# Fronts and merges between the batches of a scan network as threads of one plan; gate by channels

## The chip, the cores and the metric

The kernel runs on one core of a Trainium2 chip. A core has five engines with queues of their own, each in program order: PE (TensorE, matrix products), DVE (VectorE), ACT (ScalarE), POOL (GpSimd) and SP (SyncE, which here only issues DMA transfers). The metric is the device time of one execution in microseconds (us). Before the change it is 16153.37 us, the median of three runs (16113.97 to 16171.61).

## The reference, cut to what matters

Four layers work on x of 4 images, 64 x 64 tokens, 96 channels. Only layers 0 and 1 are touched by the change. Both are selective state-space layers over four directions of scan:

```python
xz = x @ in_proj_w.T                  # x is _gn(x), normalized by groups of 3 channels
xc, z = jnp.split(xz, 2, axis=-1)     # 192 channels each
xc = silu(depthwise_conv3x3(xc) + conv_b)
ys = [scan(xc in the order of direction k) for k in range(4)]
y = sum over k of w[k] * y_k restored to image order    # layer 0: w by token; layer 1: all 1
y = layernorm(y) * ln_g + ln_b        # over the 192 channels
y = y * silu(z)                       # the gate
x = x + y @ out_proj_w.T              # layer 1 adds an FFN of y as well
```

Layers 2 and 3 (attention, Fourier mixing, quantized FFNs) and the FFN of layer 1 come after, as stages of their own.

## The kernel before, in words

`Stream.run` does both scan layers as one stream of 8 batches: four images of layer 0, four of layer 1. A batch has 4 directions of 4 segments of 1024 tokens; a segment has 6 blocks of 32 channels by 4 groups of states, one tile of 128 x 1024 each. For such a tile DVE multiplies (L725) and scans (L732), ACT makes the decay (L720), POOL multiplies by C (L742), and PE spreads (L712) and gathers (L753). The preparation of the next segment (`prepare`) is woven into the slots of the current one by a `Weave`.

A batch needs a **front** before its scans and a **merge** after them. Both happen between batches: at the change from batch q-1 to q, `between` (called in `run` after `flush`, which drains the last tiles of q-1) runs `front` of batch q+1 and `merge` of batch q-1. Both are generators, and `between` advances them in turn, one `yield` each, with `front` left out on every third turn. So the order of instructions on every engine's queue is that of the fixed `yield`s. The first front runs alone before everything, the second just before the first scans; the last merge runs alone at the end.

`front` loads x in four strips of 1024 tokens and takes their statistics (L284), loads the strips again with one row above and below (`load_strip`, L271 and L279), normalizes them (L310), and then for each strip: `project` multiplies by the input weights, for xc by channels (L318, copied by L324 into a padded tile "spare") and for z by tokens (L330, silu in L335, stored to `z_tok` in DRAM); `convolve` runs the 9 taps as products with diagonal blocks of 32 x 32 (L356, `tile_position` of 3 x 4 places), silu (L370), turns the result to tokens (L376, L380), stores it (L391) and a product of it with the weights Ds (L393 and L395 on POOL, stored in L398).

`merge` goes through 8 chunks of 512 tokens. `fetch` loads the four directions' rows into the four buffers "h": plain loads (L422), or for directions 2 and 3 of layer 0 four indirect gathers each, issued by POOL (L426). `add` sums them (L448 with weights by token in layer 0, L450 in layer 1) and takes the statistics of the layernorm (L460 to L463). `gate` normalizes and multiplies by ln_g, ln_b and z: in layer 0 all on DVE (L472 to L474), in layer 1 the normalization on DVE (L478) and three products and sums on POOL (L480, L481). `leave` turns the chunk to channels (L492, L497); layer 0 multiplies by the output weights (L504), adds x (L506) and stores x1 (L508); layer 1 stores y1 (L500).

Pools hold what is shared: "h" 4 buffers, "hc" 3, "da" 4, "spare" 2, "dx", "x_in" and "yt" one, PSUM "t" 2 and "m", "u", "y" one each. "dt", "xs" and "sp_z" of the pool `seg` belong to `prepare` during the scans; "sp_z" also takes the front's product.

The later stages (`layer1_ffn`, `layer2`, `layer3`) are already written as threads of a `Plan`: a thread yields the engine it wants and the microseconds that this takes in a model, and `Plan.run` always goes on with the thread that can start first. `Rings` hands out buffers and takes them back.

Of the kernel before, what the change touches and what calls it, by code (L numbers as in the profile page):

```python
# [11 lines left out]
F32 = mybir.dt.float32  # L12
# [9 lines left out]
B = 4  # L22
HW = 64
# [121 lines left out]

class Layer:


    def __init__(self, s, a, pre, x_in):
# [9 lines left out]
        self.ln_g, self.ln_b = (k.t(w, [128, DI], pre + n) for n in ("ln_g", "ln_b"))  # L159
        nc.sync.dma_start(self.ln_g, a[pre + "ln_g"].to_broadcast([128, DI]))  # L160
        nc.sync.dma_start(self.ln_b, a[pre + "ln_b"].to_broadcast([128, DI]))
# [58 lines left out]
class Stream:  # L220
# [38 lines left out]
    def front(self, bt):  # L259

        k, nc, lay = self.k, self.nc, bt.lay
        x = lay.x_in[:, bt.b, :]
        bt.x_tok = k.t(self.dram, [L, DI], "x_tok")
        bt.dx_tok, bt.z_tok = (k.t(self.dram, [L, DI], n, bufs=3) for n in ("dx_tok", "z_tok"))
        stats = k.t(self.tmp, [C, NCH, 6], "gn_stats")
        strips = L // SEG
        tiles, pads = {}, {}

        def load(s):
            xs = k.t(self.core, [C, SEG], "da", bufs=4)  # L270
            nc.sync.dma_start(xs, x[:, s * SEG : (s + 1) * SEG])  # L271
            return xs

        def load_strip(s):

            tiles[s] = load(s), k.t(self.tmp, [C, 2, HW], "halo", bufs=2)
            for n, row in enumerate((s * 16 - 1, s * 16 + 16)):
                if 0 <= row < HW:
                    nc.sync.dma_start(tiles[s][1][:, n], x[:, row * HW : (row + 1) * HW])  # L279

        for c in range(strips):
            xs = load(c)
            for j in range(2):
                nc.vector.bn_stats(stats[:, 2 * c + j, :], xs[:, j * CH : (j + 1) * CH])  # L284
            yield
        for s in range(2):
            load_strip(s)
        mv, gn, d = (k.t(self.tmp, [C, n], t) for n, t in ((2, "gn_mv"), (2, "gn"), (1, "gn_d")))
        nc.vector.bn_aggr(mv, stats.rearrange("p c s -> p (c s)"))
        ps = k.t(self.ps, [C, 1], "m")  # L290
        nc.tensor.matmul(ps, self.gavg, mv[:, 0:1], start=True, stop=True)
        yield
        nc.vector.tensor_copy(gn[:, 0:1], ps)
        nc.vector.tensor_sub(d, mv[:, 0:1], gn[:, 0:1])
        nc.vector.scalar_tensor_tensor(d, d, d, mv[:, 1:2], op0=ALU.mult, op1=ALU.add)
        ps = k.t(self.ps, [C, 1], "m")
        nc.tensor.matmul(ps, self.gavg, d, start=True, stop=True)
        yield
        k.rstd(gn[:, 1:2], ps)

        def project(s):

            pad = pads[s] = self.spare()[:C].rearrange("p (h r w) -> p h r w", h=2, r=18)
            nc.gpsimd.memset(pad[:, :, :, 0 : HW + 2 : HW + 1], 0.0)
            r0 = s * 16
            xs, halo = tiles.pop(s)
            has = [r0 > 0, r0 + 16 < HW]
            edge = slice(0 if has[0] else 1, 2 if has[1] else 1)
            for v in (xs, halo[:, edge]):
                nc.vector.tensor_scalar(v, v, gn[:, 0:1], gn[:, 1:2], op0=ALU.subtract, op1=ALU.mult)  # L310
            for n in range(2):
                if not has[n]:
                    nc.gpsimd.memset(pad[:, :, n * 17, :], 0.0)
            for part in range(3):
                v = xs[:, part * CH : (part + 1) * CH] if part < 2 else halo[:, edge].rearrange("p r w -> p (r w)")
                ps = k.t(self.ps_t, [C, 2, CH], "t")[:, :, : v.shape[1]]
                for half in range(2):
                    nc.tensor.matmul(ps[:, half], lay.in_w[:, half * C : (half + 1) * C], v, start=True, stop=True)  # L318
                yield
                if part < 2:  # L320
                    rows = slice(1 + part * 8, 9 + part * 8)
                else:
                    rows = slice(edge.start * 17, 18, 17) if edge.stop == 2 else slice(0, 1)
                nc.scalar.copy(pad[:, :, rows, 1 : 1 + HW], ps.rearrange("p h (r w) -> p h r w", w=HW))  # L324
            stores = []
            for j in range(2):
                ps = k.t(self.ps_t, [128, 2, CH], "t")[:, :, : 2 * DI].rearrange("p a (b d) -> p a b d", d=DI)
                for t in range(4):
                    at = j * CH + t * 128
                    nc.tensor.matmul(  # L330
                        ps[:, t // 2, t % 2], xs[:, at : at + 128], lay.in_w[:, DI:], start=True, stop=True
                    )
                yield
                z = k.t(self.tmp, [128, 2, 2, DI], "z_rows", bufs=2)
                nc.scalar.activation(z, ps, AF.Silu)  # L335
                at = r0 * HW + j * CH
                to = bt.z_tok[at : at + CH, :].rearrange("(j p) d -> p j d", p=128)
                stores.append((to, z.rearrange("p a b d -> p (a b) d")))
            yield
            for to, z in stores:  # L340
                nc.sync.dma_start(to, z)
            if s + 2 < strips:
                load_strip(s + 2)

        def convolve(s):
            pad = pads.pop(s)

            two, one = k.t(self.ps_t, [128, 2, CH], "t"), k.t(self.ps, [128, CH], "m")
            ps = [two[:, 0, :], two[:, 1, :], one]
            for tap in range(9):  # L350
                dy, dx = divmod(tap, 3)
                for blk in range(C // GC):
                    mine = slice(blk * GC, (blk + 1) * GC)
                    for at in range(4):
# [4 lines left out]
                            pad[mine, half, j * 8 + dy : j * 8 + dy + 8, dx : dx + HW],  # L359
# [4 lines left out]

            for _ in range(3):
                yield
            xc = []
# [1635 lines left out]
```

## Time and profile before

| what | us |
|---|---|
| median of three runs | 16153.37 |
| the profiled execution, its time | 16120.49 |
| its span | 16118.7 |
| VectorE busy in it | 12944.4 (80%) |
| PE busy | 13409.0 (83%) |
| ScalarE busy | 8242.0 (51%) |
| GpSimd busy | 9957.1 (62%) |
| first scan begins | 392.5 |
| last scan ends | 12878.7 |

The span is the time from the first to the last instruction. The share of busy time of an engine is an average over stages with different limits; a table of windows gives it for one stretch, with the granted clock of PE and the share of time in which the 16 DMA engines were busy. In a table of waits, a row tells which engine's instruction waited for which, for how long in all, how often, and the longest time. In the groups of instructions, the first number behind the bar is busy time, the second the mean of one in ns, and behind the second bar stands the idle time before them with what ended it.

### The profile page before, as it was taken

To read this page: it belongs to the slowest core of one execution; us is meant where nothing else is said; L and a number is where in the kernel's file an instruction comes from. 1 tells how busy PE (TensorE), PEld (TensorE's weight loads), DVE (VectorE), ACT (ScalarE), POOL (GpSimd) and SP (SyncE) were. 2 spreads that over 40 slices of the span, in tenths; PEclk is the share of its full clock that TensorE was granted. 3 is DMA by queue.
4 is the path that set the end of the run, shared out by engine and by line. 5 is a ranking of instruction groups with operands and counts; after the bars stand their busy time and mean duration, and the time that the engine had idled before them with its cause. 6 is when DMAs were issued, how large, how long until landed. Compare 5 with 4: busy or idle time off the path is not lost. (4 is left out here: it accounts for less than half of the span.)

```text
span 16118.7 us, 190118 instructions
## 1 busy us (share of the span) xinstructions
PE 13409.0 (83%) x70447; PEld 4873.8 (30%) x70447; DVE 12944.4 (80%) x9690; ACT 8242.0 (51%) x14120; POOL 9957.1 (62%) x5025
## 2 busy tenths in 40 slices
PE   6888788878887888788878887888688869998877
PEld 3222222222222222222222222222222234443344
DVE  1989798979897989799979997999899956565555
ACT  3656465646564656466545654655466523332334
POOL 1888588858885888577757775777677730000123
PEclk8888888988888888888878888888788879998878
DMA  3333533353334333433343334333433320000132
GB/s 113 107 114 109 157 109 110 114 160 104 115 107 151 107 115 109 152 109 119 115 143 120 111 114 154 107 115 107 139 112 122 101 65 18 11 17 13 37 84 69
DMA packets 927836, 1675.23 MB, mean 104 GB/s; under 512 B 103206, under 2 KB 617515, under 8 KB 923132
## 3 DMA queue, kind: packets, MB, share of 16 engines
q1 hardware_dynamic: 890044, 1587.51, 31.7%
q0 software_dynamic: 36864, 75.55, 1.5%
q8 instruction: 558, 9.14, 0.2%
q14 instruction: 370, 3.03, 0.1%
HBM read 1308.00 MB, written 354.75 MB: 103 GB/s over the span
## 5 line engine op out<-in xcount | busy, mean ns | idle before, releaser
L742 POOL TENSOR_TENSOR hc<-h,bc 128x1024 f32<-128x1024 f32 x3072 | 7183.5, 2357 | 2112.6 <-DVE h L732 1681.4
L732 DVE TENSOR_TENSOR_SCAN h<-da,state,t 128x1024 f32<-128x1024 f32 x2304 | 5270.8, 2328 | 13.7 <-ACT da L720 9.6
L753 PE MATMUL y<-hc,gather_y 128*32 128x512 f32 x12288 | 4281.9, 689 | 671.4 <-POOL hc L742 506.2
L725 DVE TENSOR_TENSOR t<-u,bc 128x1024 f32<-128x1024 f32 x3072 | 3599.5, 1217 | 998.8 <-PE u L712 998.3
L720 ACT ACTIVATE da<-dts,L_A_logs 128x1024 f32<-128x1024 f32 x3072 | 3488.1, 1147 | 730.8 <-DMA dts<-dt_dram 438.4
L712 PE MATMUL u<-dtu,spread 32*128 32x512 f32 x3072 | 1881.2, 739 | 374.2 <-DVE t L725 370.2
L776 PE MATMUL y<-L_diag,zeros 96*32 96x256 f32 x5218 | 1751.8, 466 | 0.0
L732 DVE TENSOR_TENSOR_SCAN h<-da,t 128x1024 f32<-128x1024 f32 x768 | 1711.7, 2268 | 9.1 <-ACT da L720 8.4
L753 PEld LDWEIGHTS y<-hc,gather_y 128*32 128x32 f32 x12288 | 802.1, 117 | 2465.9 <-issue 1266.7
L644 PE MATMUL m<-xs,proj 96*128 96x512 f32 (+1 forms) x2048 | 1017.8, 620 | 116.7 <-ACT dt L653 60.4
L681 ACT COPY dt<-m 96x512 f32<-96x512 f32 x512 | 296.7, 579 | 1533.5 <-PE m L676 1533.5
L712 PEld LDWEIGHTS u<-dtu,spread 32*128 32x128 f32 x3072 | 597.9, 215 | 1440.1 <-issue 1101.2
L776 PEld LDWEIGHTS y<-L_diag,zeros 96*32 96x32 f32 x5218 | 617.7, 132 | 1284.8 <-issue 1158.4
L1186 POOL MEMSET padp<- 128x2448 f32 x32 | 68.5, 2141 | 1413.1 <-PE d L1226 1405.0
L1262 DVE SCALAR_TENSOR_TENSOR hcv<-padv,taps,hcv 128x2048 f32<-128x2048 f32 x384 | 902.2, 2349 | 22.3 <-ACT padv L1203 8.6
L1226 PE MATMUL d<-padp,diag 32*32 32x512 f32 x25600 | 886.2, 601 | 2.0 <-ACT hcp L1241 2.0
L676 PE MATMUL m<-sp_z,ident 96*96 96x512 f32 x1024 | 535.1, 605 | 192.7 <-ACT sp_z L670 192.7
L636 POOL TENSOR_TENSOR dtu<-sp_z,dtu 96x1024 f32<-96x1024 f32 x256 | 604.1, 2360 | 72.5 <-ACT dtu L634 70.1
L648 ACT ACTIVATE sp_z<-m,L_dtb 96x512 f32<-96x512 f32 x512 | 348.8, 681 | 545.4 <-PE m L644 527.7
L1226 PEld LDWEIGHTS d<-padp,diag 32*32 32x32 f32 x25600 | 483.3, 103 | 372.1 <-issue 199.3
L797 ACT COPY spare<-m 128x512 f32<-128x512 f32 x384 | 225.0, 586 | 713.3 <-PE m L794 712.9
L644 PEld LDWEIGHTS m<-xs,proj 96*128 96x128 f32 (+1 forms) x2048 | 322.6, 177 | 822.8 <-issue 314.2
(276 smaller groups left out, 15542.6 us busy)
## 6 DMA issues: line engine op xcount, KB each, us to landing
bc<-bc_dram SPq DMA_DIRECT2D x1024, 512.0 KB
dts<-dt_dram SPq DMA_DIRECT2D x768, 512.0 KB
dt_dram<-dt SPq DMA_DIRECT2D x256, 384.0 KB
h<-y_tok SPq DMA_DIRECT2D x192, 384.0 KB
y_tok<-spare SPq DMA_DIRECT2D x64, 768.0 KB
z_tok<-z_rows SPq DMA_DIRECT2D x64, 384.0 KB
x_tok<-y_rows SPq DMA_DIRECT2D x32, 768.0 KB
dx_tok<-sp_z SPq DMA_DIRECT2D x32, 768.0 KB
```

The costliest lines, as they stand in the source:

```text
L636: rest = lambda half: nc.gpsimd.tensor_add(r[:, half], z[:, half], r[:, half])
L644: nc.tensor.matmul(ps, proj[:, src, to], xs[:, src, cols], start=src == 0, stop=src == 1)
L676: nc.tensor.matmul(ps, k.ident[:C, :C], term[:, half, cols], start=at == 0, stop=at == 2)
L712: self.nc.tensor.matmul(seg.u[:, cols], self.spread[rows, :], seg.dtu[rows, half, cols], start=True, stop=True)
L720: self.nc.scalar.activation(da, seg.dts[cb], AF.Exp, scale=seg.bt.lay.neg_a[:, seg.kd, g : g + 1])
L725: self.nc.vector.tensor_mul(gr.t, gr.seg.u, self.bc[:, 0, gr.sg, :])
L732: self.nc.vector.tensor_tensor_scan(gr.h[:, order], gr.da[:, order], gr.t[:, order], start, op0=ALU.mult, op1=ALU.add)
L742: self.nc.gpsimd.tensor_mul(gr.hc, gr.h, self.bc[:, 1, gr.sg, :])
L753: nc.tensor.matmul(seg.y[at : at + GC, :], self.gather_y, gr.hc[:, part * CH : (part + 1) * CH], start=gr.sg == 0, stop=gr.sg == NSG - 1, ...
L776: self.nc.tensor.matmul(gr.seg.y[at : at + GC, :256], self.zeros, gr.seg.bt.lay.diag.rearrange("p h t c -> p (h t c)")[:, :256], start=Fal ...
L1226: nc.tensor.matmul(pc[i][j * 32 : (j + 1) * 32, :], diag[mine, ON_PE.index(t), tap, :], pad[mine, j * 8 + dy : j * 8 + dy + 8, dx : dx + H ...
L1262: nc.vector.scalar_tensor_tensor(to, win, wt, to, op0=ALU.mult, op1=ALU.add)
```

## The change

`Plan` and `Rings` move up in the file and get two additions: a thread can be `ahead`, which decides between threads that can start at the same time, and a ring can be cut out of a larger tile (`parts`). `front` and `merge` become sets of threads of such a plan, one for each strip's projection, convolution, statistics, edges, and one for each chunk's finish, with fetches and sums beside them. `between` is replaced by `side_by_side`, which puts the front of batch q+1, the merge of batch q-1 and the flush of the last scans (`ending`) into one plan; `fill` adds products with zeros where the model sees PE idle. At the start the fronts of batches 0 and 1 share a plan.

Beside the order, these things change: x is loaded once and kept in the four buffers "da"; z is projected by channels and stored as `z_t` (96 x 2 x 4096); the layernorm's scale and shift are applied by ACT, by channels, after the turn, and the gate's product follows there on DVE (layer 1's gate leaves POOL); direct rows of directions 0 and 1 get two buffers of their own, cut from "dt", and z two from "xs"; the bank "u" of layer 0 is held until x is added, since the output product goes into its first half; the borders of "spare" are zeroed by DVE. The loop of the convolution's products is not changed.

```diff
+    def side_by_side(self, ahead, behind=None, flush=None):
+        k, nc = self.k, self.nc
+        plan, rings = Plan(), Rings(k)
+        self.ended, self.idle = False, None
+        def ending():
+            yield "none", 1.2
+            if flush:
+                flush()
+            self.idle = k.t(self.ps_y, [128, CH], "y")
+            self.ended = True
+            yield "PE", 4.0
+        def fill():
+            if self.idle is not None:
+                data = self.layers[0].diag.rearrange("p h t c -> p (h t c)")[:, :384]
+                nc.tensor.matmul(self.idle[:GC, :384], self.zeros, data, start=True, stop=True)
+        plan.fill = fill
+        if behind:
+            plan.add(self.merge(behind, plan, rings))
+        for bt in ahead:
+            plan.add(self.front(bt, plan, rings, None if bt is ahead[0] else ahead[0]), 1)
+        plan.add(ending())
+        plan.run()
+        self.idle = None
...
-            for _ in self.front(batches[0]):
-                pass
+            self.side_by_side(batches[:2])
...
-                    flush()
+                    q = batches.index(seg.bt)
+                    if q:
+                        self.side_by_side(batches[q + 1 : q + 2], batches[q - 1], flush)
                     before = []
                     seg.bt.y_tok = [k.t(self.dram, [L, DI], f"y_tok{kd}") for kd in range(ND)]
-                    self.between(batches.index(seg.bt), batches)
...
-            flush()
-            for _ in self.merge(batches[-1]):
-                pass
+            self.side_by_side([], batches[-1], flush)
```

`Plan.run` and the start of `Plan.add`, as they are after the change (`Rings.take` and `give` as before, but for `parts`):

```python
    def add(self, work, ahead=None):
        at = self.current.at if self.current else 0.0
        if ahead is None:
            ahead = self.current.ahead if self.current else 0
        self.threads.append(SimpleNamespace(work=work, at=at, wants=("none", 0.0), ahead=ahead))
    ...
                start = max(th.at, self.free.get(th.wants[0], 0.0))
                if best is None or (start, -th.ahead) < (best[0], -best[1].ahead):
                    best = start, th
            start, th = best
            engine, us = th.wants
            if engine == "PE" and self.fill:
                for _ in range(int((start - self.free.get("PE", start)) / 1.0)):
                    self.fill()
            if engine != "none":
                self.free[engine] = start + us
                now = max(now, start)
            th.at = start + us + (0.2 if us else 0.0)
```

In `front` (one strip's load with its statistics, and z; `convolve` has the same matmuls, with `take`, `give` and costs between them):

```diff
+        def measure(s, st):
+            st.x = yield from take(self.core, [C, SEG], "da", 4)
+            yield "SP", 0.1
+            nc.sync.dma_start(st.x, x[:, s * SEG : (s + 1) * SEG])
+            yield "none", 2.5
+            yield "DVE", 1.4
+            for j in range(2):
+                nc.vector.bn_stats(stats[:, 2 * s + j, :], st.x[:, j * CH : (j + 1) * CH])
...
+            def outer(j):
+                cols = slice(j * CH, (j + 1) * CH)
+                ps = yield from take(self.ps_t, [C, 2, CH], "t", 2)
+                yield "PE", 1.8
+                for half in range(2):
+                    w = lay.in_w[:, DI + half * C : DI + (half + 1) * C]
+                    nc.tensor.matmul(ps[:, half], w, xs[:, cols], start=True, stop=True)
+                z = yield from take(self.tmp, [C, 2, CH], "z_rows", 2)
+                yield "ACT", 1.1
+                nc.scalar.activation(z, ps, AF.Silu)
...
+                nc.sync.dma_start(bt.z_t[:, :, at : at + CH], z)
...
+        works = [work for s, st in enumerate(strips) for work in (project(s, st), convolve(s, st))]
+        yield from plan.together(works)
```

In `merge`:

```diff
+        def fetch(kds):
+            if kds[0]:
+                yield lambda: self.ended
+            for n in range(NCH):
+                for kd in kds:
+                    if kd < 2:
+                        g = yield from take(None, None, "rows", 2)
+                    else:
+                        g = yield from take(self.core, [128, T, DI], "h", 4)
+                    if not lay.ordered or kd < 2:
+                        yield "SP", 0.1
+                        nc.sync.dma_start(g, rows_of(bt.y_tok[kd], n))
+                    else:
+                        yield "POOL", 5.0
+                        for j in range(T):
...
+                    plan.add(landed((n, kd), g))
...
+        def finish(n, acc, mv):
+            plan.add(load(("z", n), None, None, "z", 2, bt.z_t[:, :, cols_of(n)]))
+            yield "ACT", 1.0
+            nc.scalar.activation(mv[:, :, 1], mv[:, :, 1], AF.Sqrt, bias=k.eps)
+            yield "DVE", 1.7
+            nc.vector.reciprocal(mv[:, :, 1], mv[:, :, 1])
...
+                nc.vector.tensor_scalar(acc[:, j], acc[:, j], m, r, op0=ALU.subtract, op1=ALU.mult)
+            give(mv)
+            ps = yield from take(self.ps_u, [C, 2, CH], "u", 1)
...
+            yield "PE", 2.4
...
+            yt = yield from take(tmp, [C, 2, CH], "yt", 1)
+            yield "ACT", 1.4
+            for half in range(2):
+                g, b = lay.ln_g[:, half : half + 1], lay.ln_b[:, half : half + 1]
+                nc.scalar.activation(yt[:, half], ps[:, half], AF.Identity, bias=b, scale=g)
+            yield lambda: ("z", n) in got
+            z = got.pop(("z", n))
+            yield "DVE", 1.1
+            nc.vector.tensor_mul(yt, yt, z)
...
             if not lay.ordered:
-                yield
-                nc.sync.dma_start(self.y1[:, bt.b, cols].rearrange("(h c) t -> c h t", c=C), yt)
+                give(ps)
...
+            yield "PE", 1.6
             for half in range(2):
-                nc.tensor.matmul(ps, self.out_w[:, half, :], yt[:, half, :], start=half == 0, stop=half == 1)
...
+                nc.tensor.matmul(ps[:, 0], self.out_w[:, half, :], yt[:, half, :], start=half == 0, stop=half == 1)
+            give(yt)
+            yield lambda: ("x", n) in got
+            xs = got.pop(("x", n))
+            yield "DVE", 0.75
+            nc.vector.tensor_add(xs, xs, ps[:, 0])
+            give(ps)
```

## The prediction

> **What bounds the kernel now.** The change touches only the code that runs between the batches of the two scan layers, so I first separated those stretches. On the timeline of VectorE I took, at each change of batch, the end of the last scan (L732) and the start of the next batch's first one:
>
> ```profile
> 1802.11 4.58 DVE L732 TENSOR_TENSOR_SCAN h<-da,state,t 128x1024 f32<-128x1024 f32 x2
> ...
> 2013.48 4.45 DVE L732 TENSOR_TENSOR_SCAN h<-da,t 128x1024 f32<-128x1024 f32 x2
> ```
>
> From 1806.7 to 2013.5 us nothing is scanned: 206.8 us. The seven gaps are 206.8, 206.4, 209.0, 209.5 (each merges a layer 0 batch beside a front), 187.2, 185.0 (layer 1 merge beside a front) and 129.8 (merge alone), 1333.7 us of a span of 16118.7. Outside them lie the last merge, 135 us up to the first L1195 matmul of the next stage at 13013.9, and the start, where the first scan begins at 392.5. Everything else, 8 scan phases of 1357 to 1414 us and the last 3100 us, keeps its instructions. Next, the busy time by engine in these stretches (columns: PE, weight loads, VectorE, ScalarE, GpSimd, granted clock, DMA share, GB/s):
>
> ```profile
> 100.00:392.00 292.00, 192.02 (x2122) 103.98 (x2120) 23.70 (x45) 95.94 (x204) 38.25 (x21) 0.80 0.44 131
> 1807.00:1827.00 20.00, 5.55 (x18) 1.92 (x18) 2.69 (x6) 2.45 (x3) 10.06 (x10) 0.62 0.90 283
> ...
> 1807.00:2013.00 206.00, 118.51 (x1150) 63.75 (x1150) 110.02 (x303) 59.26 (x90) 87.13 (x75) 0.75 0.64 192
> 8224.00:8411.00 187.00, 104.62 (x1119) 61.55 (x1120) 86.78 (x159) 59.35 (x92) 65.31 (x36) 0.71 0.66 199
> 11391.00:11521.00 130.00, 26.14 (x92) 15.55 (x93) 80.30 (x139) 18.03 (x26) 51.86 (x26) 0.52 0.65 198
> ```
>
> The second line is the first 20 us of the third. Over a gap no resource is full. The fullest is DMA: 0.64 of 206 us is 132 us of all 16 engines, ahead of PE (118) and VectorE (110). So the gap is set by waits on one another. The waits of that stretch:
>
> ```profile
> ACT ln_mv L463 <- DVE ln_mv L461: 50.0, 6, 29.7
> POOL h L426 <- DVE hc L448: 48.2, 6, 13.1
> ...
> POOL sp_z L393 <- DMA sp_z<-L_weight_x: 33.7, 2, 32.4
> ...
> PE m L291 <- ACT ln_mv L463: 32.0, 1, 32.0
> PE t L318 <- DVE da L310: 29.4, 4, 12.5
> ```
>
> A gather waits 48 us until a sum frees one of four buffers; PE waits 29 us for a strip that was loaded late. These are waits made by the fixed alternation of two generators, front and merge, on in-order queues. Two groups of the same stretch matter for the sums:
>
> ```profile
> L426 POOL DMA_INDIRECT h<-y_tok,scan_inv x64 | 73.1, 1143 | 76.4 <-DVE hc L448 48.2 <-issue 14.3 <-DMA y_tok<-spare 5.8
> L473 DVE SCALAR_TENSOR_TENSOR hc<-hc,ln_mv,L_ln_b 128x192 f32<-128x192 f32 x32 | 13.4, 419 | 1.1
> L472 DVE SCALAR_TENSOR_TENSOR hc<-hc,ln_mv,L_ln_g 128x192 f32<-128x192 f32 x32 | 13.0, 406 | 0.0
> L474 DVE TENSOR_TENSOR hc<-hc,z 128x768 f32<-128x768 f32 x8 | 7.7, 965 | 0.3
> ```
>
> **What the Trainium skill says.** "DMA: Bandwidth & Descriptors", Issuing engines are not separate DMA queues: transfers of all queues run on the same 16 engines. So I add the bytes of SP and POOL. The trace agrees: in the gap the gather packets (4608 B in 251 ns) and the 768 B packets (41 ns) both move 18 to 19 B/ns per engine. "Trainium Architecture — The Big Picture" (What this means for kernel authors): VectorE and GpSimd share one SBUF port pair under an exclusive lock. The trace agrees: an L450 sum takes 960 ns alone and 1515 ns on average in the lone merge, beside GpSimd's gate. "TensorE: Matmul & The Clock Gate", Part 1: an idle PE runs at half clock until it has been busy for some microseconds. Agrees: eight L318 records take 7.09 us after idling (115.4) and 3.60 us warm (126.3).
>
> **The change part by part**, for a layer 0 gap.
>
> *Transfers.* x is no longer loaded twice: four loads of 384 KB go, 39.55 MB become 37.98. z's bytes stay; its rows become 2 KB instead of 768 B, which at 18.6 against 18.9 B/ns per engine is worth nothing. 39.55 MB cost 132.7 us of 16 engines, so 37.98 cost 127.4. SP still issues about 80 transfers of some 0.45 us, 36 us.
>
> *VectorE.* L472 to L474 go (34.1 us). In come 32 normalizations of 128x192 (1.25 us for four, as L478 has undisturbed: 10.0), 8 products of 96x1024 (estimate from L474 by columns, 1.3 each: 10.3) and the border memsets taken from POOL (1.3). 110 becomes 98.
>
> *PE.* z by channels is 4 matmuls of 512 columns a strip, 3.6 us warm like L318, instead of L330's 2.87: +2.9 us. The convolution keeps its loop: L356 already writes twelve positions, 8.2 us a strip. So "twelve tiles at once" brings nothing. Fillers between matmuls (384 columns each) take only what the plan believes idle; the clock should rise from 0.75 and save about 3 us on each cold projection. About 115.
>
> *ScalarE.* Two activations of 512 columns with scale and bias (0.68 each, from L648) replace one copy of 1.01: +2.8; silu on 1024 columns instead of 768: +1.5. Table loads: 13 of 1.283 us now; not fewer than about 5, and at most 20 if every Sqrt falls between two silus. I take 15. About 66. I cost it at nothing, since 127 us of transfers cover it; on the path it would be 7 us a gap, 42 in all.
>
> *POOL.* 64 gathers at 0.95 plus 0.30 to issue are 80 us, the four products 14. They can start once the last rows have landed, 13 us in: 107. No longer behind the sums' four shared buffers: gathers have the four to themselves, direct rows two others (carved from "dt" and "xs", free by then).
>
> *Order.* Fronts, sums and finishes become threads; each engine takes what the plan says is ready. x is loaded ahead of the flush, so its statistics no longer wait 14 us. New waits: a chunk's transposes for the bank "u" (behind them on PE stand the front's matmuls), a product for z (behind it on VectorE the sums). Left over after the plan, prepare of the next segment needs "dt" and "xs" back, but it starts as late today.
>
> So every engine sums to less than DMA, and I take DMA as the bound, at the share it holds in the first 20 us of today's gap (0.90): 127.4 / 0.90 = 141.5 us. After the last rows come the finish of one chunk (transposes 1.1, two activations 1.3, product 1.3, out_w 2.0, sum 0.7, handovers of about 0.3: 7.4), u (2.0) and two products (2.4): 12. **153.5 us**, against 207.9 on average: four gaps, -218.
>
> Layer 1 with a front: 37.30 - 1.57 = 35.73 MB; at 123.3 us for 37.30 that is 118.1, / 0.90 = 131, and 10 behind it: 141 against 186.1. POOL's gate (47 us, L480 and L481) goes. VectorE's sums fall from 43 to 31 without the lock, and its product brings 10. Two gaps, -90.
>
> Merge alone: a chunk now takes 12.4 us (L478 starts at 12921.27, 12933.71, 12946.14), a chain of sums slowed by the lock, POOL's gate and z's late load. After: VectorE 4 x 0.96 + 2.06 + 0.15 + 1.25 + 1.3 = 8.6; transfers 7 x 393 KB = 2.75 MB, 9.0 us, 10.0 at 0.90. 7 intervals x 2.4 = 17, twice: -34.
>
> Start: a front alone takes 103 us (99 to 203) and 110 (281 to 391), at 20 us a strip, of which PE works 17. Two in one plan: PE 3.6 + 0.6 + 3.6 + 8.2 + 2.5 = 18.5 a strip, 8 strips 148, 17 to begin, 8 to end: 173 instead of about 213. Then dts' load, until now hidden behind the second front, stands open for some 9 us: -31.
>
> Sum: -218 - 90 - 34 - 31 = -373. The profiled execution took 16120.5 us (span 16118.7 and 1.8 around it), 0.2% under the median of 16153.4. Taken from the median: **15,780**.
>
> **The rivals.** *Plan too optimistic (0.22).* The plan counts 2.5 us for a landing; now x takes over 6 us under load (VectorE waits 23.8 us for it in three waits). Loads issued just in time then stop a whole in-order queue, and SP, where a store waiting for its producer holds every load behind it (today L508 waits 29.5 us for L448). DMA's share would stay near 0.72: 127 / 0.72 + 12 = 189 and 118 / 0.72 + 10 = 174 for the gaps, -10 for each merge alone, -15 at the start: -75 - 24 - 35 = -134, 16,020. Against it: x, the edges and the rows are asked for as soon as a buffer is free.
>
> *Slower (0.09).* The single "u" bank of PSUM is now held from the transposes through out_w to the final sum; today it is free after one copy. Its chain is 7.4 us a chunk unhindered, and the front wins ties, so each of two PE visits can stand behind a convolution of 8.2 us or more. The first chunk is ready about 27 us in. At (208 - 27) / 8 = 22.6 us a chunk a layer 0 gap gains nothing. Layer 1 lacks out_w and isn't hit; if its gaps only stay as they are, start and lone merges still bring 65, and from 26 us a chunk the kernel is slower by 0.3%. At 28 us: 27 + 224 = 251, 4 x 43 - 65 = +107, 16,260. Against it: convolutions are 33 us of a gap, so an average visit waits 1 to 3 us.
>
> *No change (0.05).* The plan's gain on the gaps is eaten by its fillers and stalls: 16,153. The measurement tells about 0.3% from no change.
>
> *Better (0.10).* DMA full throughout: 139 and 128 for the gaps, 24 for each lone merge, 45 at the start: -276 - 116 - 48 - 45 = -485, 15,668.
>
> **How the numbers follow.** The forecast itself has 0.54, from 15,700 to 15,900. The range holds it, the better case and nearly all of the optimistic plan's: 15,640 to 16,080; some 0.17 lies above and 0.03 below. Faster: 0.54 + 0.10 + 0.20 of the second case = 0.84; the rest of that case and the fourth give 0.07 for the same; slower 0.09.
>
> **What would show it.** Gaps of 140 to 165 us (layer 0) and 130 to 155 (layer 1), with a DMA share near 0.85; the gathers 80 to 100 us from first to last with little wait for L448's successor; POOL under 20 us in layer 1 gaps; scan phases unchanged within 15 us each. Wrong if the share stays at 0.7 with queues waiting for landings, if "u" transposes wait long for the bank's last sum, or if scan phases move.

## The result, and the profile after

The changed kernel takes 16,023.4 us, the median of four runs (15,991.1 to 16,028.5), beside 16,154.8 for the kernel before (now the median of four): a ratio of 0.992 with an interval of 0.9895 to 0.9941. It is 131 us faster, where 373 had been forecast. A second measurement of the same kernel, on the chip called B below, gave 16,009.4 us and 0.989 (0.988 to 0.991).

The profiled execution took 15,991.1 us. VectorE's timeline at the first change of batch (start, length, instruction, and in brackets the idle time ahead of it with what ended it):

```profile
1812.67 4.57 DVE L900 TENSOR_TENSOR_SCAN h<-da,state,t 128x1024 f32<-128x1024 f32 x2
1840.04 1.41 DVE L603 SCALAR_TENSOR_TENSOR hc<-dt,fuse,dx 128x192 f32<-128x192 f32 x4 [22.80 <-DMA dx<-dx_tok]
...
1997.16 4.45 DVE L900 TENSOR_TENSOR_SCAN h<-da,t 128x1024 f32<-128x1024 f32 x2
```

The gap is 180 us instead of 207, and it begins with 22.8 us in which VectorE has nothing. The seven gaps are 179.9, 178.7, 179.5, 183.7, 169.5, 167.9 and 106.1. The stretch after the last scan fell from 3239.9 to 3215.7. The first scan begins at 408.5 instead of 392.5, and the eight scan phases together last 11,199.7 us instead of 11,152.7. Gaps -168, end -24, start +16, phases +47: -129, the difference of the two spans. The busy times by engine, in the columns of before; the fourth line is the third layer 0 gap:

```profile
100.00:408.00 308.00, 221.78 (x2115) 97.22 (x2114) 33.42 (x57) 97.87 (x210) 36.88 (x12) 0.81 0.40 121
1817.00:1837.00 20.00, 8.89 (x28) 2.82 (x28) 0.24 (x1) 2.65 (x4) 12.52 (x12) 0.72 0.97 290
1817.00:1997.00 180.00, 133.46 (x1169) 60.52 (x1170) 102.39 (x278) 68.64 (x110) 84.25 (x70) 0.86 0.76 223
4998.40:5177.90 179.50, 133.30 (x1172) 60.84 (x1172) 101.87 (x278) 68.87 (x110) 86.10 (x70) 0.85 0.70 205
8176.00:8346.00 170.00, 113.45 (x1114) 55.43 (x1114) 83.17 (x175) 64.99 (x100) 18.34 (x6) 0.80 0.71 210
11317.00:11422.00 105.00, 65.95 (x184) 23.79 (x184) 66.00 (x146) 20.84 (x33) 2.39 (x2) 0.73 0.83 241
```

DMA's share of the first layer 0 gap rose from 0.64 to 0.76, where the forecast had 0.90 ahead of a tail of 12 us, which is 127.4 / 153.5 = 0.83 over the gap. In the four layer 0 gaps the share is 0.76, 0.77, 0.70 and 0.68. The first 20 us are full (0.97); the loss comes later. POOL fell to 18 us in the layer 1 gap, as forecast. Some waits of the first gap (who, for whom, us in all, times, longest):

```profile
DVE hc L603 <- DMA dx<-dx_tok: 22.8, 1, 22.8
DVE halo L421 <- DMA halo<-in_x: 19.8, 2, 15.6
...
DVE yt L651 <- ACT yt L647: 15.1, 4, 7.6
...
PE u L638 <- DVE x_in L668: 8.0, 5, 5.2
```

VectorE's two longest waits are now landings: it stands 42.6 us for dx and for halo rows. The longest waits of SyncE's queue:

```profile
SPq L550 <- DMA x<-x_in: 22.3, 7, 4.6
SPq L575 <- DVE ln_mv L627: 16.3, 3, 9.2
```

SyncE stands 22.3 us because the next x can't be loaded into x_in before the store of x1 from it has landed. The order of its queue at the start of the gap (start, time to issue):

```profile
1824.65 0.39 SPq L983 DMA_DIRECT2D y_tok<-spare  x1
...
1826.96 2.00 SPq L369 DMA_DIRECT2D da<-in_x  x4
```

The store of y_tok belongs to the flush; the loads of x come behind it. And the groups, busy time and mean ns:

```profile
L697 PE MATMUL y<-L_diag,zeros 96*32 96x384 f32 x48 | 22.1, 604 | 0.0
L630 DVE TENSOR_SCALAR hc<-hc,ln_mv 128x192 f32<-128x192 f32 x32 | 16.8, 588 | 0.3
L651 DVE TENSOR_TENSOR yt<-yt,xs 96x1024 f32<-96x1024 f32 x8 | 9.7, 1217 | 15.1 <-ACT yt L647 15.1
```

### The profile page after: what moved, and what is told of

The parts are those of the page before. It is cut to its first block, busy times and chain, and to the rows that moved or that the text cites. A ratio compares the mean times of both kernels' runs of the same rounds, so it can differ in the third digit from the quotient of the medians.

```text
span 15989.3 us, 190160 instructions
## 1 busy us (share of the span) xinstructions
PE 13629.1 (85%) x70689; PEld 4868.9 (30%) x70689; DVE 12884.4 (81%) x9642; ACT 8295.0 (52%) x14192; POOL 9763.9 (61%) x4881
## 5 line engine op out<-in xcount | busy, mean ns | idle before, releaser
L1265 POOL MEMSET padp<- 128x2448 f32 x32 | 68.6, 2144 | 1481.9 <-PE d L1305 1376.1
L1305 PEld LDWEIGHTS d<-padp,diag 32*32 32x32 f32 x25600 | 483.5, 103 | 370.6 <-issue 197.9
```

The lines of the kernel that those rows point to most:

```text
L1305: nc.tensor.matmul(pc[i][j * 32 : (j + 1) * 32, :], diag[mine, ON_PE.index(t), tap, :], pad[mine, j * 8 + dy : j * 8 + dy + 8, dx : dx + H ...
```

## The experiments

The theory after the result: *stalls*, that is, instructions put into an in-order queue before their data had landed. The rival: *transfers*, that is, 38 to 40 MB that can't move faster. Later a third joined them, about the start. The runs lie on four chips, A to D; a kernel is compared with the kernel before on its own chip. The first two rows stand for the two profiles of this document, whose chip is not on record. In us: first scan, mean of the four layer 0 gaps, mean of the two layer 1 gaps beside a front, lone merge (the seventh gap, which has no front), sum of the eight scan phases.

| run | chip | ratio to before | first scan | layer 0 | layer 1 | lone | phases |
|---|---|---|---|---|---|---|---|
| before | | 1 | 392.5 | 207.9 | 186.1 | 129.8 | 11,153 |
| after | | 0.992 | 408.5 | 180.5 | 168.7 | 106.1 | 11,200 |
| before_again | A | | 391.0 | 207.8 | 185.8 | 128.9 | 11,202 |
| gate_alone | A | 1.004 | 401.5 | 222.9 | 189.8 | 110.5 | 11,241 |
| halo4 | A | 0.992 | 410.0 | 195.3 | 186.3 | 107.4 | 11,231 |
| old_start | A | 0.989 | 413.7 | 181.6 | 170.5 | 110.0 | 11,219 |
| copies | A | 0.995 | 414.5 | 194.9 | 179.1 | 108.1 | 11,211 |
| landings | A | 0.986 | 402.8 | 172.6 | 151.0 | 101.4 | 11,248 |
| landings_act | A | 0.986 | 404.3 | 169.2 | 153.7 | 102.8 | 11,204 |
| landings_xin3 | A | 0.984 | 406.2 | 168.1 | 152.3 | 102.8 | 11,142 |
| after_again | B | 0.989 | 406.5 | 184.6 | 168.9 | 107.2 | 11,244 |
| xin3_again | B | 0.982 | 407.1 | 165.8 | 153.1 | 102.6 | 11,140 |
| less_again | B | 0.983 | 408.5 | 162.5 | 152.9 | 102.7 | 11,217 |
| nofill_again | B | 0.983 | 386.0 | 171.2 | 150.5 | 102.8 | 11,137 |
| less_bytes | C | 0.990 | 410.3 | 207.1 | 151.1 | 102.8 | 11,217 |
| landings_6us | C | 0.990 | 412.7 | 222.3 | 145.9 | 103.1 | 11,191 |
| no_fill | C | 0.986 | 392.7 | 213.3 | 151.3 | 102.3 | 11,138 |
| combined | C | 0.992 | 406.0 | 211.3 | 154.2 | 103.4 | 11,193 |
| final | D | 0.987 | 392.8 | 206.4 | 151.8 | 103.7 | 11,248 |
| final_6us | D | 0.988 | 392.5 | 222.5 | 145.1 | 101.3 | 11,200 |

The intervals of the ratios are 0.001 to 0.004 to each side.

**The two measurements that set the scale.** No edit; the kernels before and after once more.

> The kernel before once more, for the scan phases, whose code no run here changes. Their sum was 11,152.7 us before and 11,199.7 after, and 11,211 to 11,248 in four variants. If this is variation from run to run, this run lies anywhere from 11,140 to 11,250; if the change slows the scans (by what it leaves in queues or in the clock), it lies at 11,140 to 11,170 again.

> The changed kernel itself, once more. If the convolution that issues one instruction each 0.70 us (26 to 30 us lost in each layer 0 gap of less_bytes, landings_6us, no_fill and combined, which ran on another chip than the runs before) belongs to that chip and not to the kernels, then wherever this run shows layer 0 gaps of 178-184 us, xin3_again shows 164-177, and both show the slow convolution or both do not. If it belongs to the order of the later kernels, this run has none in any case.

The phases of the kernel before came out 49 us longer, those of the changed kernel 44 longer, and over all runs they lie between 11,137 and 11,248 without regard to what was edited. Three other kernels that ran twice have sums equal within 3 us, but their single phases differ by up to 56. Whole executions of one kernel vary as much: 22 of the kernel before on chip A took 16,116 to 16,227 us. The +47 us of the result is thus no effect that these runs can tell from variation. The gaps repeat better: 180.5 and 184.6 on average for the changed kernel, 207.9 and 207.8 for the one before. Differences of 2 or 3 us between single gaps are not read below.

**One part alone.** In the kernel before, z by channels, and scale, shift and gate after the turn; the fixed order stays:

```diff
-                    nc.vector.scalar_tensor_tensor(acc[:, j], acc[:, j], m, lay.ln_g, op0=ALU.subtract, op1=ALU.mult)
-                    nc.vector.scalar_tensor_tensor(acc[:, j], acc[:, j], r, lay.ln_b, op0=ALU.mult, op1=ALU.add)
-                nc.vector.tensor_mul(acc, acc, z.pop())
+                nc.vector.tensor_scalar(acc[:, j], acc[:, j], m, r, op0=ALU.subtract, op1=ALU.mult)
...
-            nc.scalar.copy(yt, ps)
+                nc.scalar.activation(yt[:, half], ps[:, half], AF.Identity, bias=b, scale=g)
+            nc.vector.tensor_mul(yt, yt, z.pop(0))
```

> The kernel before with one part of the change: z by channels, and the scale, shift and gate of the layernorm by channels after the turn (no threads, no plan; x is still loaded twice; the sum of x in the bank y as before). If the operations bring the gain: layer 0 gaps 206-209 to 180-190, layer 1 gaps 186 to about 170, the lone merge 130 to 105-112. If the order by the plan brings it: layer 0 gaps 198-208, layer 1 gaps 178-187, the lone merge above 118. The start stays at 392 within 5 us in both.

It is slower than before, 1.004 (1.002 to 1.005). Its windows of the first layer 0 gap, the first layer 1 gap and the lone merge, and a wait of the first:

```profile
1826.00:2046.60 220.60, 135.00 (x1118) 64.71 (x1118) 96.47 (x272) 66.06 (x100) 91.28 (x76) 0.71 0.60 183
8321.50:8508.20 186.70, 101.91 (x1086) 53.22 (x1086) 81.08 (x168) 62.41 (x98) 17.44 (x12) 0.74 0.65 198
11509.60:11620.10 110.50, 26.69 (x93) 15.74 (x94) 67.24 (x147) 21.61 (x34) 2.75 (x2) 0.52 0.75 230
```

```profile
DVE yt L489 <- ACT yt L488: 49.1, 8, 11.5
```

VectorE lost 13 us of work in the layer 0 gap and POOL 48 in layer 1's, and no gap beside a front became shorter: in the fixed order the product stands at once behind ScalarE's activation, and VectorE waits 49 us for it (45 in the layer 1 gap). Neither expectation holds for these gaps. Layer 0's became 15 us longer, so there the rest of the change (the order, x loaded once, buffers of their own) brings more than the whole gain. Only the lone merge gains by the operations: 19 of the 24 us. There a sum of VectorE takes 958 ns instead of 1515, now that GpSimd does no gate beside it. The start missed both expectations as well: 401.5 beside 391.0 on the same chip. The two fronts, from the first load of x to the last store, took 107 and 111 us instead of 103 and 109, so z by channels accounts for some 6 of these 10 us.

**Halo rows.**

```diff
-            halo = yield from take(self.tmp, [C, 2, HW], "halo", 2)
+            halo = yield from take(self.tmp, [C, 2, HW], "halo", 4)
```

> Only the ring of halo rows has four buffers instead of two. Theory of stalls (what a gap lost, it lost to instructions that stood in an in-order queue before their data had landed): the 19.8 us that VectorE waits for halo rows in a layer 0 gap go, a part of it turns up at the next wait, and the gaps beside a front fall from 180 to 162-172 us (layer 0) and from 169 to 158-167 (layer 1); in the start, where 47 us are spent on halo rows, the first scan comes at 375-395 us instead of 408. The lone merge stays at 106. In all 80 to 130 us less. Theory of transfers (the 16 DMA engines cannot be driven above a share of 0.7 to 0.76 by this mixture, and halo rows are late because of that): all gaps within 3 us of the changed kernel's, since the same bytes move.

The theory of stalls, put in this simple form, falls. The time is that of the changed kernel (0.992), and the profiled execution, 77 us above the median of its five, shows longer gaps, not shorter ones. Its SyncE queue:

```profile
SPq L550 <- DMA x<-x_in: 30.3, 7, 9.3
SPq L575 <- DVE ln_mv L627: 29.9, 4, 18.1
```

In the first gap VectorE no longer waits for halo rows, but 26.4 us for PE at the padded tile "spare"; SyncE stands longer at x_in and at the direct rows, and holds the loads behind it. The first scan, expected at 375 to 395, came at 410.0. More buffers in one place moved the stall to the next.

**Real landings.** In the planner, a thread that asks for a delay ran its next step at the delay's beginning. So for every thread that waits for it, a load of rows, dx, z or halo counted as landed when issued, and the flush, put off by 1.2 us in the text, came first. In this run the delay passes before the next step:

```diff
+            now = max(now, start)
+            if engine == "none" and us:
+                th.at, th.wants = start + us, ("none", 0.0)
+                continue
             if engine != "none":
                 self.free[engine] = start + us
-                now = max(now, start)
```

> In the planner a delay on no engine (a landing, the 1.2 us ahead of the flush) really passes before the next step of its thread; in the changed kernel that step ran at the delay's beginning. Theory of stalls: the loads of x, dx and the first direct rows are issued ahead of the flush's store, so VectorE's first wait of a layer 0 gap falls from 22.8 to about 12 us, and the gap from 180 to 165-175. Theory of transfers: order does not matter, gaps within 3 us of 180 and 169. A third possibility is that honest landings of 2.5 us reorder later instructions for the worse, which would show as a shorter first wait and no shorter gap.

SyncE's queue, VectorE's first waits, and the window of the first gap:

```profile
1810.71 4.50 SPq L372 DMA_DIRECT2D da<-in_x  x4
...
1820.61 2.07 SPq L986 DMA_DIRECT2D y_tok<-spare  x1
```

```profile
DVE gn_stats L376 <- DMA da<-in_x: 17.0, 4, 16.0
...
DVE halo L424 <- DMA halo<-in_x: 11.6, 2, 11.3
```

```profile
1806.00:1982.00 176.00, 134.33 (x1164) 61.13 (x1165) 105.82 (x277) 68.31 (x110) 85.04 (x70) 0.85 0.79 227
```

The loads of x now stand ahead of the flush's store. The first wait is 16 us instead of 22.8, the halo wait 11.6 instead of 19.8. Layer 0 gaps fall by 8 to 12 us against the two profiles of the changed kernel, layer 1 gaps by 18, the lone merge by 5: order matters, and the pure theory of transfers falls. The kernel is at 0.986.

**SyncE's queue**, on top of real landings: x_in with three buffers, measured twice, or ScalarE as the issuer of its own stores.

```diff
-                plan.add(load(("x", n), tmp, [C, CH], "x_in", 1, lay.x_in[:, bt.b, cols_of(n)]))
+                plan.add(load(("x", n), tmp, [C, CH], "x_in", 3, lay.x_in[:, bt.b, cols_of(n)]))
```

> As the run with real landings, and x_in of the merge has three buffers instead of one, so that the load of the next x need not wait for the store of x1 to land. Theory of SyncE's queue (a load whose buffer is not free stands in SyncE's queue, and every later transfer behind it: 14.8 us in the first gap of that run, 7.4 us a chunk in its tail): layer 0 gaps fall by 5 to 12 us from 176, 173, 166, 175; layer 1 gaps, which do not use x_in, stay at 150 to 152 within 2 us. Theory of transfers: layer 0 gaps within 3 us.

> Real landings and three x_in buffers, once more, beside the changed kernel on the same chip. Theory: 0.990 to 0.994 of the changed kernel's time, layer 0 gaps 164-177, layer 1 gaps 150-155. If the first run was lucky in its scan phases (their sum was 11,142 us, 57 under the changed kernel's), the gaps repeat and the time is 15,880 to 15,950.

```diff
-            yield "SP", 0.1
-            nc.sync.dma_start(to(bt.x_tok), flat)
+            nc.scalar.dma_start(to(bt.x_tok), flat)
```

> As the run with real landings, and ScalarE, which produces them, issues the stores of z_t and x_tok (12 in a gap) instead of SyncE. Theory of SyncE's queue: the 10 us and more that it stands at these stores go, and the loads behind them come earlier; gaps beside a front fall by 4 to 10 us, in layer 0 and layer 1 alike. Theory of transfers: within 3 us. Against both: if issuing costs ScalarE more than about 1 us each, gaps rise.

With three buffers the layer 0 gaps are 168.1 and 165.8 (172.6 before the edit), the layer 1 gaps 152.3 and 153.1 (151.0, untouched by it): 5 to 7 us a gap, the lower end of what the theory of the queue said. This is an average: three gaps fell by 9 to 16 us, and the third rose by 7 to 11, in both runs. SyncE's wait at x_in is gone; in the first gap on chip B it stands 30.7 us for sums to free the buffers of direct rows instead. On chip B this kernel is at 0.982 (0.980 to 0.984), beside 0.989 for the changed kernel. ScalarE's stores: 3 us in layer 0, nothing in layer 1, which the noise of gaps doesn't tell from none.

**Bytes**, added to the changed kernel and taken away from the kernel with three x_in:

```diff
+            for n in range(2):
+                to = k.t(self.dram, [C, SEG], "copied", bufs=8)
+                nc.sync.dma_start(to, x[:, s * SEG : (s + 1) * SEG])
```

> Adds eight copies of 384 KB within DRAM to every front, 3.1 MB beside the 38 MB of a layer 0 gap, which nothing waits for. Theory of transfers: at 127 us of all engines for 38 MB they are 10.5 us more, so a gap beside a front grows by 11 to 15 us, six times 11 to 15 in all. Theory of stalls: they fill time in which the engines idle; the gaps grow by 0 to 5 us. The lone merge, which has no copies, stays at 106 in both.

```diff
-            if lay.ordered:
-                yield "SP", 0.1
-                nc.sync.dma_start(dxs, to(lay.weight_x))
```

> As the run with real landings and three x_in buffers, and layer 0's fronts do not load the weights of Ds by token: the four products take layer 1's weights from SBUF instead. It leaves out the weights of that product, so dx and the result are other numbers; 3.1 MB of the 38 MB of a layer 0 gap go. Theory of transfers (what is left of a gap is transfers at a share of about 0.83): layer 0 gaps from 168 on average to 154-159. Theory of order (queues wait on one another, bytes are hidden): layer 0 gaps 164-169. Gaps of layer 1 merges beside a front (150 to 154) have no such load and stay within 3 us; but the gap that merges the last layer 0 batch makes a layer 1 front, so it stays too, and three of the four should move.

> The run without layer 0's weights of Ds once more, now beside the kernel that it differs from. It leaves out those weights, so dx and the result are other numbers. Transfers bind: layer 0 gaps that make a layer 0 front are 9 to 14 us shorter than xin3_again's. Order binds: within 4 us, or longer.

The copies cost 10 to 14 us a gap beside a front on average (2 to 24 in single gaps), and 1 or 2 in the lone merge that has none: the size that the theory of transfers gave. But they also stand ahead of halo loads in SyncE's queue, and VectorE's wait for halo rows grew by 4 to 10 us in every gap beside a front, so this run doesn't part the bytes from the order. The windows of the first gap, three x_in and then without the weights, both on chip B:

```profile
1812.60:1979.50 166.90, 136.80 (x1167) 62.20 (x1168) 103.56 (x277) 68.64 (x110) 84.49 (x70) 0.84 0.80 239
```

```profile
1817.10:1979.70 162.60, 129.91 (x1160) 58.70 (x1160) 102.87 (x278) 68.85 (x110) 87.19 (x70) 0.87 0.76 226
```

The three gaps that lose the weights' load are 162.6 on average, against 168.5 for the same three over both runs with it (4, 1 and 12 us, gap by gap); the fourth, which makes a layer 1 front, is 162.0 against 162.3. So 3.1 MB, some 10 us of all engines, are worth 6 us, and the share of the first gap falls to 0.76: about half of what a pure bound would give, between the two expectations. This edit, too, takes the wait for a load away with its bytes. What is left of a gap is most likely both: bytes in some stretches, order in others; no run parts the two.

**The start and the fillers.** First the order of before at the start, then PE without fillers:

```diff
-            self.side_by_side(batches[:2])
+            self.side_by_side(batches[:1])
...
+            self.side_by_side(batches[1:2])
```

> Only the start has the order of the kernel before: front of batch 0 alone, the first prepare, then front of batch 1. Theory: the changed start is longer because the two fronts in one plan do not overlap (both need all four buffers of x), so that the loads of states and of dt lie open behind it. Then the first scan comes at 388-398 us instead of 408.5, all gaps stay within 2 us, and the kernel gains 10 to 20 us. Rival: the 16 us come from slower fronts (z by channels, fewer things in flight); then the first scan stays at 405-412.

```diff
-        plan.fill = fill
```

> As the run with real landings and three x_in buffers, without the products with zeros that fill PE's idle stretches. If they keep PE's clock up, the granted clock in the gaps falls from about 0.85 towards the 0.75 of the kernel before, and gaps grow by 3 to 10 us. If they only stand in the way of real products, the gaps shrink by 2 to 6 us. The prediction counted them at nothing: within 2 us.

> The run without fillers once more, beside the kernel that it differs from. Clock theory: layer 0 gaps 3 to 10 us longer than xin3_again's at a granted clock of about 0.75. Prediction: within 2 us.

In old_start the second front was put ahead of the loads of states and dt, so these lay open still (VectorE waits 46.6 us for the states); it could not show what it was to show. The run called combined, which has it behind those loads, with ScalarE's stores and three x_in, tells more:

> Real landings, three x_in buffers, ScalarE's stores, and the start in the old order with the second front behind the loads of states and dt. First scan at 396-404 us instead of 406, since those loads are hidden behind the second front (about 10 us in the changed kernel's start); gaps as in the runs before, 165-172 and 150-155; in all 15,860 to 15,910. If it is the fronts themselves that are slower, the first scan stays above 405.

The first scan came at 406.0, where less_bytes on the same chip had 410.3: the order of the start is worth 4 us at most, since combined has ScalarE's stores as well, and the expectation missed. The fillers are worth far more: without them 386.0 on chip B against 407.1, the same kernel but for the fillers. The filler's group on PE up to the first scan in the run with fillers on chip B, and two windows there and without fillers (nofill_again):

```profile
L700 PE MATMUL y<-L_diag,zeros 96*32 96x384 f32 x68 | 34.0, 628 | 0.8 <-DVE fuse L1117 0.8
```

```profile
100.00:200.00 100.00, 84.12 (x1007) 40.23 (x1006) 15.71 (x28) 31.67 (x63) 10.35 (x3) 1.00 0.41 123
200.00:316.00 116.00, 95.83 (x1059) 44.92 (x1058) 11.31 (x27) 39.99 (x69) 17.20 (x5) 0.94 0.51 155
```

```profile
100.00:200.00 100.00, 78.33 (x1002) 39.69 (x1001) 14.60 (x28) 36.64 (x66) 11.88 (x4) 0.98 0.45 135
200.00:316.00 116.00, 78.06 (x1005) 39.90 (x1006) 10.47 (x27) 36.09 (x93) 15.71 (x5) 0.82 0.46 141
```

In the first window PE has a clock of 0.98 without help and is busy 78%; in the second the fillers raise the clock from 0.82 to 0.94, and the start is still longer with them. They are 34 us of products with zeros, wherever the plan took PE for idle. Eight of the 68 stand ahead of the first front, whose first load of x is issued at 104.3 instead of 99.1; the second front's last store is issued at 311.9 instead of 297.5. In layer 0 gaps the fillers pay on average: 171.2 without, 165.8 with, at a granted clock of 0.76 against 0.86, though the third gap is 2 us longer with them. In layer 1 gaps they cost 3 us (150.5 without, 153.1 with), no more than the noise of gaps. In the lone merge the clock goes from 0.52 to 0.76 and the time stays (102.8 and 102.6).

**Landings of 6 us, and the last kernel.** The planner's landings raised from 2.5 to 6.0 us; then three x_in with fillers only where a merge runs, with either landing.

> As the run with real landings and three x_in buffers, with landings counted as 6 us instead of 2.5 in the planner, nearer to what loads take under load. If the rest of the stalls comes from landings that the model takes too short, VectorE's waits for halo rows (10.3 us in that run's first gap) and for gathers shrink and gaps beside a front fall by another 4 to 10 us. If the transfers bind, they stay within 4 us.

> Real landings, three x_in buffers, and fillers only where a merge runs (none in the start, where 68 of them took 34 us of a PE at full clock). The first scan comes at 386 us within 4 as in nofill_again, against 406-407 with fillers; layer 0 gaps 160-176 as in xin3_again, layer 1 gaps 150-156. In all about 20 us under xin3_again's 0.982 of the kernel before: 0.9805, unless the chip shows the slow convolution (then layer 0 gaps of 200 and more).

> The same with landings counted as 6 us. On the other chip this made the gaps of layer 1 merges 144 and 148 us, 3 to 7 shorter than with 2.5 us; layer 0 could not be read there. If late landings are what is left of the stalls, layer 0 gaps fall by 4 to 10 us from the other kernel's and the kernel is the faster by 20 to 40 us; if not, layer 0 gaps are equal or longer and only the 10 us of layer 1 show.

Layer 1 gaps fall to 145 us (151 to 152 with 2.5), twice. Layer 0 gaps are longer. The first scan of final is at 392.8, as in no_fill: the start's loss is the fillers'. On chip D final is at 0.987 (0.985 to 0.990) and final_6us at 0.988. Neither ran on a chip like A or B; the best that was measured is three x_in on chip B, 15,867 us, 0.982. All six runs on chips C and D have layer 0 gaps of 206 to 223 us; the last section tells what they share. So whether longer landings help layer 0, and whether final is better than three x_in on a chip like B, stays open.

## Why the prediction was right and wrong

The direction held, and the range held the time. The forecast did not: of 373 us came 131.

- *DMA at 0.90 of its time.* This is the step that failed. A share read in the fullest 20 us of the old gap was taken for the whole of the new one. With the 12 us behind it, it means 0.83 over a layer 0 gap and 0.84 over a layer 1 gap; measured were 0.76, 0.77, 0.70 and 0.68, and 0.71. Four gaps 27 us above the 153.5 and two 28 above the 141 are 163 of the 244 us that the profiled execution lacks. The bytes are the smaller part, and too few only in the first two gaps: 40.1 MB instead of 37.98, of which a fourth store of dx_tok and a load of dts, which now fall into the window, are 1.3; they cost 137 us of all engines, not 127. The third and fourth gap move 36.8 and 36.9 MB in 125 us, fewer than forecast (the forecast took the first gap's bytes for all four; the old third and fourth moved 37.1 MB), and yet are as long.
- *The order, "x is loaded ahead of the flush".* Wrong, and the largest cause that the runs show for the low share. On SyncE's queue the flush's store came first; the delay in the code did not delay. The run with real landings took back 8 to 12 us of each layer 0 gap and 18 of each layer 1 gap, and three x_in buffers 5 to 7 more in layer 0. With both, the share of the first two gaps is 0.80 to 0.82, near the 0.83, and they take 164 to 167 us, 12 more than forecast, of which some 7 are bytes (133.5 us of all engines instead of 127, at 0.83). In the third gap it stays at 0.70 and 0.71, and that is not explained.
- *The rival of a plan too optimistic.* It came near this mechanism: landings that the plan takes too short, and SyncE held by a store, though not a delay that doesn't delay. It gave 16,020, beside 16,023 measured. That the number fits so well is luck: its gaps, 189 and 174, were 9 and 5 us too long and its lone merges 14 each, its start was 31 too short, and the 47 us of the phases were not in it.
- *Layer 1 gains because POOL's gate goes.* POOL went to 18 us as said, and VectorE's sums there from 1457 to 955 ns in gate_alone, as forecast. But gate_alone has gaps of 190: in the fixed order a wait for ScalarE took the place of the gain. It needed the new order.
- *Lone merges, -17 each.* They gave 24 each; 19 of them come with the operations alone.
- *The start, -31.* It was +16, 47 us worse, and two terms failed. The fillers, priced as harmless, are 21. The other is the overlap: two fronts in one plan were to take 173 us, and without fillers they still take 198 (nofill_again, from the first load of x at 99.1 to the second front's last store at 297.5). In the kernel the second front waits until the first has projected all its strips (`yield lambda: first.to_project == 0`), and its loads of x are issued only at 197.9, so the two hardly overlap. This is read from the code and the trace; no run left that wait out.
- *VectorE 98, ScalarE 66.* 102.4 and 68.6. The normalization took 0.59 us instead of 0.31 (L630; 0.38 in the lone merge, where GpSimd is busy for 2 of 105 us), the product 1.22 instead of 1.3. Both engines stay far below the 180 us of the gap.
- *"u" as a new bound.* PE waited 8 us for it in the first gap, its weight loads 11.5: rightly a small chance.
- *"Twelve tiles at once brings nothing".* Right: 108 recorded products of the convolution, half a strip's, take 4.5 us in both kernels where nothing interrupts them.
- *Scan phases unchanged.* The 47 us they seem to cost are no more than what two runs of one kernel differ by (44 and 49).

The 244 us are thus: gaps beside a front 163, start 47, phases 47, the two lone merges -14.

## What to carry to other kernels

A planner that orders in-order queues is only as good as its model: check on the issuing queue that a delay in the text is a delay in the queue, before counting on what should come first. A sum of busy time over the largest engine is a floor; price a gap by the share that its resource holds over the whole of it, not in its fullest 20 us. And filler work has a price to be measured stretch by stretch: the same fillers gained 5 us a layer 0 gap on average, nothing in the lone merge, and lost 21 in the start.

## What the runs showed of the hardware that was not expected

On chips C and D the first convolution of every layer 0 gap runs at one recorded instruction each 0.70 us, or a multiple, for 18 to 30 us. The convolution's line alone, in 26 us of the first gap, in less_bytes (chip C) and in xin3_again (chip B); columns PE, weight loads, clock, DMA:

```profile
1841.00:1867.00 26.00, 12.61 (x18) 1.78 (x16) 0.57 0.70 188
```

```profile
1843.00:1869.00 26.00, 8.37 (x216) 5.04 (x216) 0.87 0.75 206
```

Eighteen recorded products against 216, which are a strip's. The kernels less_bytes and no_fill ran on both kinds of chip, and only on C did they show it, so it belongs to the chip or its state. In the stretches of less_bytes, no_fill and final that were followed, GpSimd's gathers were running, and in the first convolutions the slow issue ended 3 to 6 us after the last gather of an unbroken row, about 20 of which ran beside it. Layer 1 gaps and the start, which have no such gathers, show none. On B the same products ran at full speed beside the same gathers. What the two share was not found, and neither the kernel before nor the changed one was profiled on C or D; the kernel before took 16,235 and 16,272 us there, 0.5 and 0.7% more than on A and B.

Over the same 3072 scans, the phases differed by up to 111 us between runs, in steps of about 3.3 us for each stretch of 24 scans. No edit explains it, and its cause stays open.
